# A two-layer graph network in float32 on one core: score products in another order, a second layer with 256 columns a graph, and a bias added by an accumulating transfer

## The chip, the cores and the metric

The kernel runs on one core of a Trainium2 chip. The time is that of the device for one execution, in microseconds (us). In the profile PE is TensorE, PEld its weight loads, DVE VectorE, ACT ScalarE, POOL GpSimd and SP the engine that issues most transfers.

## The reference

The input x has 64 graphs of 256 nodes with 512 features, adj a 256 x 256 weight matrix for each graph, all in float32. Two layers follow each other, each on a normed and rectified copy of x and added to x:

```python
h = maximum(layernorm(x), 0)
q, k, v = h @ Wq.T + bq, h @ Wk.T + bk, h @ Wv.T + bv
w = adj * exp(q @ k.T)
x = x + (w / w.sum(axis=2)) @ v

h = maximum(layernorm(x), 0)
A = adj + eye
d = A.sum(-1) ** -0.5
x = x + (A * d[:, None] * d[None, :]) @ (h @ W + b)
```

## The kernel before, in words

The kernel works on pairs of graphs (G = 2, NP = 32 pairs). A pair has four row blocks of 128 rows (TB = 4); block t = nb * G + g is row half nb of graph g. x of three pairs, and adj of two, are held in SBUF.

Every large product is done with seven products of half size instead of eight (a Winograd scheme): four quarters of each operand and sums of them go in, and sums of the products come out. `seven_products` (L342) does this for three stages, each with 28 matmuls of 128x128 by 256 columns: `key_side` (pm_g: h times the merged query and key weight), `values` (pm_v) and the second layer's weight product (pm_w). A product `product(bank, ...)` adds into one of three PSUM banks, 0, 1, 0, 1, 2, 1, 2 in this order, and between two uses of a bank a DVE or ACT operation reads it. The callbacks `then_first`, `then_u2`, `then_c11`, `then_u3` put other work on the engines behind the operation that reads the bank.

`attend` (L488) does the scores the same way, with products of 128 columns (pm_s, L500) in four banks. `first` (sA), `u2` and `u3` (sU) and `c22` (sC) are the sums on the way. `weights(kb, qb, scores)` then takes ACT's exponential (L519) for two graphs and multiplies on DVE by the transposed adjacency (L520, called the mask below); wT holds the result. The fourth part of `attend` multiplies wT by v (pm_o, L548), takes the reciprocal of the row sum (L556) and adds to x (L558). Because the row weights add up to one, the value bias can be added to x itself: `add_value_bias` (L738) does so before L558 with four additions on POOL (L741).

`transposed_adjacency` (L468) makes aT with DVE's 32x32 transposes from a copy of adj (aq) whose blocks a transfer has put in place; aT is laid out as (key half, query half, graph, query). After the first layer POOL adds the identity to aT's diagonal blocks (L801). `convolve` (L600 on) then forms pm_l (L611) with aT as the moving operand, 128 columns a matmul, two graphs side by side in a bank, and feeds the result as seven parts (yS) to pm_w. Its results are scaled by degree and added to x by DVE (L646) and POOL (L653).

Other names in the steps: `key_sums` (L329, gS) and `feature_sums` (L315, hS) make the operand sums, on POOL but for the first pair's hS; `weight_sums` (L155) makes those of a weight; `find_terms` calls `key_terms` (hc, L282), a row sum on DVE; `degrees` (L560) and `weighted_degrees` (ad, L579) give d; `scale_offset` (L245) measures mean and variance (L251) and ends in roots on POOL (L242); `normed` (L264) is ACT's normed copy h.

Each engine works through its own list in order. The order is that in which the program names the operations, except that `tc.issue_after(x)` puts what is named in it behind the instruction x, and that a planner (the tile framework) moves instructions of independent chains past each other when the program is built. In the middle of the program, for each pair p, the stages follow as attend(p), key side and values of p + 1, second layer of p; so pm_s, pm_o, pm_g, pm_v, pm_l, pm_w, and again. The start does key side and values of pair 0 with work of pair 1 among them (`project_first_pair`, L764), and the end has two second layers.

Of the kernel before, what the change touches and what calls it, by code (L numbers as in the profile page):

```python
# [9 lines left out]
F32 = mybir.dt.float32  # L10
# [6 lines left out]
def kernel(  # L17
# [93 lines left out]
    bkT = const.tile([P, DC], F32, tag="bkT", name="bkT")  # L111
    bv_all = const.tile([P, D], F32, tag="bv", name="bv_all")
    b1_all = const.tile([P, D], F32, tag="b1", name="b1_all")
# [14 lines left out]
    load_a(1)  # L128
    nc.sync.dma_start(bv_all, bv.partition_broadcast(P))
    w1_view = w1.rearrange("(j t p) (i f) -> i j p t f", p=P, t=2, f=HD)  # L130
# [198 lines left out]
    def key_sums(p, gT):  # L329

        a11, a21 = gT[:, 0:2, 0:N], gT[:, 0:2, N:NT]
        a12, a22 = gT[:, 2:4, 0:N], gT[:, 2:4, N:NT]
        gS = p1.tile([P, 3, 2, N], F32, tag="gS", name=f"gS_{p}")
        s1, s2, s4 = (gS[:, i] for i in range(3))
        nc.gpsimd.tensor_tensor(s1, a21, a22, add)
        nc.gpsimd.tensor_tensor(s2, s1, a11, sub)

        nc.gpsimd.tensor_tensor(a21, a11, a21, sub)
        nc.gpsimd.tensor_tensor(s4, a12, s2, sub)
        return (a11, a12, a22, s1, s2, a21, s4)  # L340
# [88 lines left out]

    def values(p, parts, then_first, then_u2, then_c11, then_u3):  # L430
        a1, s2, s3 = (temp(tag, f"v{p}") for tag in ("A1", "U2", "U3"))

        def block(i, g):
            return v[:, 2 * g : 2 * g + 2, i * (HD + 1) : i * (HD + 1) + HD]

        def first(pm):
            with tc.issue_after(nc.scalar.copy(a1, pm).ins):
                then_first()

        def u2(pm):  # L440
            with tc.issue_after(nc.vector.tensor_tensor(s2, pm, a1, add).ins):  # L441
                then_u2()

        def c11(pm):
            with tc.issue_after(nc.scalar.copy(block(0, 0), pm).ins):
                then_c11()

        def u3(pm):
            with tc.issue_after(nc.vector.tensor_tensor(s3, pm, a1, add).ins):  # L449
                then_u3()  # L450

        return seven_products(
            f"v_{p}",
            v_set,
            parts,
            True,
            first=first,
            u2=u2,
            c11=c11,
            u3=u3,  # L460
            c22=lambda pm: nc.vector.tensor_tensor(block(1, 1), pm, s3, add),
            c21=lambda pm: nc.vector.tensor_tensor(block(1, 0), pm, a1, add),
            c12=lambda pm: nc.vector.tensor_tensor(block(0, 1), pm, s2, add),
        )

    def transposed_adjacency(p):
        a = a_tiles[p]

        aT = p2.tile([P, NB, NB, G, P], F32, tag="aT", name=f"aT_{p}")
        if p > 0:  # L470
            in_view = q_tiles[p].rearrange("p kt (g j) r -> p kt g (j r)", g=G)
            for kt in range(NB):
                for g in range(G):
                    nc.vector.transpose(aT[:, kt, :, g, :], in_view[:, kt, g])
            return aT
        for g in range(G):
            pt = ps_m.tile([P, NB, NB, P], F32, tag="pm", name=f"pt_a_{p}_{g}")
            for kb in range(NB):
                for qb in range(NB):
                    nc.tensor.transpose(  # L480
                        pt[:, kb, qb, :], a[:, qb * G + g, ts(kb, P)], ident
                    )
            nc.scalar.copy(aT[:, :, :, g, :], pt)
        return aT

    def attend(p, h_parts, g_parts, ks, aT):
# [27 lines left out]

        def weights(kb, qb, scores):
            block = wT[:, kb, qb]
            for g in range(G):
                t = kb * G + g
                nc.scalar.activation(block[:, g], scores[:, g], AF.Exp, bias=ks[:, t : t + 1])  # L519
            nc.vector.tensor_tensor(block, block, aT[:, kb, qb], mult)  # L520

# [3 lines left out]
        nc.vector.tensor_tensor(u2, pm1, first, add)  # L525
        product(0, a12, b21, False)
        weights(0, 0, pm0)
        product(1, s3, t3, False)
        nc.vector.tensor_tensor(u3, pm1, first, add)
        pm2 = product(2, s1, t1)  # L530
        nc.vector.tensor_tensor(c22, pm2, u3, add)
        pm3 = product(3, a22, t4)
        nc.vector.tensor_tensor(u3, pm3, u3, add)
        weights(1, 0, u3)
        weights(1, 1, c22)
        product(2, s4, b22, False)
        nc.vector.tensor_tensor(u2, pm2, u2, add)
        weights(0, 1, u2)
        for qb in range(NB):
# [60 lines left out]
    def convolve(p, h, aT, d, moved, then_t4, then_first, then_u3):  # L600
# [4 lines left out]

        def aggregate(fh, qb):
            pm = ps_m.tile([P, 2, N], F32, tag="pm", name=f"pm_l_{p}_{qb}_{fh}")
            for fi in range(2):
                for g in range(G):
                    for jb in range(NB):  # L610
                        nc.tensor.matmul(  # L611
                            pm[:, fi, ts(g, P)],
                            h[:, jb * G + g, ts(2 * fh + fi, P)],
                            aT[:, jb, qb, g, :],
                            start=jb == 0,
                            stop=jb == NB - 1,
                        )
            return pm
# [17 lines left out]
        def block(i, g):  # L636
            return xt[:, 2 * g : 2 * g + 2, ts(i, HD)]

        def scaled(dst, pm, g, plus=None):

            for r in range(2):
                dr_ = d[:, 2 * g + r : 2 * g + r + 1]
# [50 lines left out]
        if p == NP - 1:  # L693
            for i, nb in ((0, 0), (1, 1), (1, 0), (0, 1)):
                rows = out[G * p : G * p + G, ts(nb, P), ts(i, HD)].rearrange("g p k -> p g k")
                nc.sync.dma_start(rows, block(i, nb))
        else:
# [40 lines left out]
    def add_value_bias(p):  # L738
        for t in range(TB):
            xh = x_tiles[p][:, t, :]  # L740
            nc.gpsimd.tensor_tensor(xh, xh, bv_all, add)  # L741

# [3 lines left out]
    def project(p, then_g):  # L746
        keys[p], last = key_side(p, parts[p], then_g, ahead(measure, p + 1), nothing)
        key_parts[p] = key_sums(p, keys[p])
        if p == 1:
            with tc.issue_after(last):  # L750
                weight_sums(w1_set, w1_21)
        last = values(
# [11 lines left out]
    def project_first_pair(v21):  # L764
# [6 lines left out]
        def during_g2():  # L771
            turn_blocks(1)
            deg[1] = degrees(1)
            with tc.issue_after(last_root[0]):
                add_value_bias(0)

        keys[0], _ = key_side(0, parts[0], lambda: norm_features(1), during_g, during_g2)
        key_parts[0] = key_sums(0, keys[0])
        last = values(
            0,  # L780
            parts[0],
            then_first=lambda: move_first_half(1),
            then_u2=lambda: find_terms(1),
            then_c11=lambda: move_second_half(1),
            then_u3=nothing,
        )
# [8 lines left out]
    def first_layer(p):  # L795
        attend(p, parts[p], key_parts[p], terms[p], aTs[p])


        for t in range(TB):
            diag = aTs[p][:, t // G, t // G, t % G]  # L800
            last = nc.gpsimd.tensor_tensor(diag, diag, ident, add)  # L801
# [107 lines left out]
```

## Time and profile before

| | us |
|---|---|
| median of 3 runs | 1868.14 |
| lowest and highest | 1866.42, 1868.26 |
| the profiled execution | 1865.99 |
| its span, first to last instruction | 1864.2 |
| PE busy, of the span | 1846.3 |
| DVE, POOL, ACT busy | 1346.6, 818.8, 802.2 |
| mean granted TensorE clock (1 is full) | 0.999 |

The page gives each engine's busy time and the costliest groups of instructions; the chain of waits follows the end of the program back to what released it; the timeline gives instructions in order of time. A float32 matmul of the program appears as two records. The ends of matmuls are modelled, so that their recorded length (379 ns for 256 columns) is longer than the distance of two of them; the distance is read from stretches of the chain. A wait is put down to the releaser that ended last in the records, which need not be the one that counted.

### The profile page before, as it was taken

The numbers are of one execution on the slowest core, as the hardware profiler recorded it, in microseconds if no ns is written. First come the engines' busy times: TensorE is split into PE (matmuls) and PEld (weight loads), VectorE is DVE, ScalarE is ACT, GpSimd is POOL, SyncE is SP. The second block draws the span as 40 slices with busy tenths as digits, with TensorE's granted clock in tenths as the row PEclk, the third lists the DMA queues.
The fourth block names the chain that finished last, engine by engine and source line by source line (L and its number), as shares of the span: only waits on it lengthen the run. The fifth ranks groups of instructions, "written<-read, shape, count | busy, mean of one in ns | idle before, by whom it ended". The sixth has DMA issues, their size and how long they took to land.

```text
span 1864.2 us, 28019 instructions
## 1 busy us (share of the span) xinstructions
PE 1846.3 (99%) x10370; PEld 1668.7 (90%) x10370; DVE 1346.6 (72%) x3160; ACT 802.2 (43%) x1476; POOL 818.8 (44%) x967
## 2 busy tenths in 40 slices
PE   9899999999999999999999999999999999999999
PEld 8799998999898999989998989999899989899988
DVE  6877777776776777777767767777777677677755
ACT  4344434344434444343444344444434443444422
POOL 3634345444345343454443453434544434534342
PEclk9999999999999999999999999999999999999999
DMA  8122022221122221222211222212222112222001
GB/s 209 29 74 74 23 57 73 70 74 49 43 63 68 74 74 23 57 74 69 74 49 43 63 69 74 74 23 57 74 69 74 49 44 63 68 74 74 7 23 46
DMA packets 207449, 115.14 MB, mean 62 GB/s; under 512 B 149712, under 2 KB 170192, under 8 KB 207312
## 3 DMA queue, kind: packets, MB, share of 16 engines
q1 hardware_dynamic: 206192, 112.29, 22.6%
q8 instruction: 82, 1.34, 0.3%
q14 instruction: 55, 0.45, 0.2%
q10 hardware_dynamic: 1056, 1.05, 0.2%
q0 software_dynamic: 64, 0.00, 0.1%
HBM read 79.70 MB, written 33.62 MB: 61 GB/s over the span
## 4 chain that ended last, share of the span: by engine, by line
PE 94%; DVE 3%; POOL 1%; ACT 1%; issue 1%; DVEq 0%; POOLq 0%
PE pm_g L359 21%; PE pm_w L359 21%; PE pm_v L359 20%; PE pm_l L611 12%; PE pm_o L548 12%; PE pm_s L500 7%; DVE wT L520 2%; POOL aT L801 1%; ACT wT L519 1%; PE pm_mT L177 1%; DVE hc L282 0%; PE pm_run_in L169 0%; DVE ad L579 0%; PE pt_h L302 0%; DVE w_set L157 0%
## 5 line engine op out<-in xcount | busy, mean ns | idle before, releaser
L359 PE MATMUL pm_w<-w_set,yS 128*128 128x256 f32 x1792 | 392.1, 379 | 0.0
L359 PEld LDWEIGHTS pm_w<-w_set,yS 128*128 128x128 f32 x1792 | 338.0, 190 | 44.6
L312 ACT COPY hT<-hq 32x512 f32<-32x512 f32 x496 | 305.5, 616 | 35.5 <-DVE hq L293 29.7
L653 POOL TENSOR_TENSOR x<-x,A_w 128x512 f32<-128x512 f32 x32 | 40.6, 1268 | 525.2 <-ACT A_w L644 525.2
L359 PE MATMUL pm_v<-v_set,hT 128*128 128x256 f32 x1024 | 242.0, 379 | 2.5 <-DVE U_v L441 2.5
L359 PE MATMUL pm_g<-hT,m_set 128*128 128x256 f32 x1024 | 236.7, 379 | 0.0
L611 PEld LDWEIGHTS pm_l<-aT,h_b 128*128 128x128 f32 x2048 | 233.7, 192 | 1.7
L611 PE MATMUL pm_l<-aT,h_b 128*128 128x128 f32 x2048 | 233.8, 275 | 0.0
L548 PE MATMUL pm_o<-v,wT 128*128 128x257 f32 (+1 forms) x1024 | 228.0, 379 | 0.4 <-DVE wT L520 0.4
L359 PEld LDWEIGHTS pm_v<-v_set,hT 128*128 128x128 f32 x1024 | 194.6, 190 | 29.4 <-DVE U_v L441 2.9
L359 PEld LDWEIGHTS pm_g<-hT,m_set 128*128 128x128 f32 x1024 | 194.5, 190 | 27.0 <-issue 0.5
L548 PEld LDWEIGHTS pm_o<-v,wT 128*128 128x128 f32 x1024 | 190.9, 189 | 27.5 <-DVE wT L520 1.4
L359 PE MATMUL pm_v<-v_set,hS 128*128 128x256 f32 x768 | 178.3, 382 | 3.4 <-DVE U_v L449 3.4
L359 PE MATMUL pm_g<-hS,m_set 128*128 128x256 f32 x768 | 181.3, 379 | 0.0
L359 PEld LDWEIGHTS pm_v<-v_set,hS 128*128 128x128 f32 x768 | 146.9, 191 | 23.8 <-DVE U_v L449 3.6
L741 POOL TENSOR_TENSOR x<-x,bv_all 128x512 f32<-128x512 f32 x128 | 164.5, 1313 | 0.0
L359 PEld LDWEIGHTS pm_g<-hS,m_set 128*128 128x128 f32 x768 | 145.4, 190 | 20.5 <-DVE U_g L399 0.3
L646 DVE SCALAR_TENSOR_TENSOR x<-pm_w,irr_d,x 128x256 f32<-128x256 f32 x256 | 110.9, 474 | 71.8 <-PE pm_w L359 71.8
L520 DVE TENSOR_TENSOR wT<-wT,aT 128x256 f32<-128x256 f32 x128 | 104.5, 816 | 52.8 <-ACT wT L519 52.8
L653 POOL TENSOR_TENSOR x<-x,U_w 128x512 f32<-128x512 f32 x64 | 81.3, 1270 | 105.6 <-DVE x L646 105.6
L268 ACT ACTIVATE h_b<-x,nb_b,rs_b 128x512 f32<-128x512 f32 x128 | 93.8, 803 | 62.6 <-POOL nb_b L261 62.6
L391 ACT COPY A_g<-pm_g 128x512 f32<-128x512 f32 x32 | 18.8, 586 | 232.9 <-PE pm_g L359 232.2
(137 smaller groups left out, 2688.5 us busy)
## 6 DMA issues: line engine op xcount, KB each, us to landing
x<-in_x_dram SPq DMA_DIRECT2D x64, 512.0 KB, 5.3
out_dram<-x SPq DMA_DIRECT2D x62, 512.0 KB, 3.5
a<-in_adj_dram SPq DMA_DIRECT2D x64, 256.0 KB, 2.9
aq<-in_adj_dram SPq DMA_DIRECT2D x124, 128.0 KB, 3.7
drow<-dflat SPq DMA_DIRECT2D x32, 256.0 KB, 4.8
wk_rows<-in_L_gnn_Wk_w_dram SPq DMA_DIRECT2D x2, 512.0 KB, 6.8
wq_rows<-in_L_gnn_Wq_w_dram ACTq DMA_DIRECT2D x2, 512.0 KB, 7.5
wv_rows<-in_L_gnn_Wv_w_dram SPq DMA_DIRECT2D x1, 1024.0 KB, 11.0
```

The source lines that it names most:

```text
L177: nc.tensor.matmul(pm, wk_rows[:, oc, ts(dc, P)], wq_rows[:, oc, ts(half, HD)], start=oc == 0, stop=oc == DC - 1,)
L268: nc.scalar.activation(h[:, t, :], x_tiles[p][:, t, :], AF.Relu, bias=nb[:, t : t + 1], scale=rd[:, t : t + 1],)
L312: last = nc.scalar.copy(dst[j * Q : (j + 1) * Q, i], src[i * Q : (i + 1) * Q, j])
L359: nc.tensor.matmul(banks[bank][:, r, :], left[:, ts(r, P)], right, start=start and r == 0 and dt == 0, stop=r == 1 and dt == 1, skip_group ...
L391: with tc.issue_after(nc.scalar.copy(a1, pm).ins):
L500: nc.tensor.matmul(banks[bank][:, g, :], left[:, dt, ts(g, P)], right[:, dt, ts(g, P)], start=start and g == 0 and dt == 0, stop=g == 1 an ...
L520: nc.vector.tensor_tensor(block, block, aT[:, kb, qb], mult)
L548: nc.tensor.matmul(pm[:, 0:width], wT[:, kb, qb, g, :], v[:, kb * G + g, lo : lo + width], start=kb == 0, stop=kb == NB - 1,)
L611: nc.tensor.matmul(pm[:, fi, ts(g, P)], h[:, jb * G + g, ts(2 * fh + fi, P)], aT[:, jb, qb, g, :], start=jb == 0, stop=jb == NB - 1,)
L646: last = nc.vector.scalar_tensor_tensor(dst[:, r, :], pm[:, r, :], dr_, plus[:, r, :], mult, add)
L653: last = nc.gpsimd.tensor_tensor(block(i, g), block(i, g), more, add).ins
L741: nc.gpsimd.tensor_tensor(xh, xh, bv_all, add)
```

## The change

The parts are these. `attend` takes the third bank's first product and the second bank's second one earlier, splits `weights` into exponentials and masks, and puts the masks behind the sums of later products. aT is laid out as (key half, graph, query), so that pm_l takes 256 queries of one graph in a matmul, with half as many matmuls, and a bank of pm_l holds one graph; the second layer's results belong to a graph instead of a row half. The value bias is added to x by one transfer from memory with an addition at its target, issued by POOL, instead of by four additions. In the start, the key sums of pair 0 go from POOL to DVE, those of the second layer's weight come from pair 1 forward into the values of pair 0, and find_terms(1) moves to the end of these.

```diff
-    bv_all = const.tile([P, D], F32, tag="bv", name="bv_all")
-    nc.sync.dma_start(bv_all, bv.partition_broadcast(P))
...
# key_sums
-        nc.gpsimd.tensor_tensor(s1, a21, a22, add)
+        eng = nc.vector if p == 0 else nc.gpsimd
+        eng.tensor_tensor(s1, a21, a22, add)
...
# values
+        def c22(pm):
+            with tc.issue_after(nc.vector.tensor_tensor(block(1, 1), pm, s3, add).ins):
+                then_c22()
...
# transposed_adjacency
-        aT = p2.tile([P, NB, NB, G, P], F32, tag="aT", name=f"aT_{p}")
+        aT = p2.tile([P, NB, G, N], F32, tag="aT", name=f"aT_{p}")
         if p > 0:
-            in_view = q_tiles[p].rearrange("p kt (g j) r -> p kt g (j r)", g=G)
             for kt in range(NB):
-                for g in range(G):
-                    nc.vector.transpose(aT[:, kt, :, g, :], in_view[:, kt, g])
+                nc.vector.transpose(
+                    aT[:, kt].rearrange("p g q -> p (g q)"),
+                    q_tiles[p][:, kt].rearrange("p j r -> p (j r)"),
+                )
...
# attend
-        def weights(kb, qb, scores):
-            block = wT[:, kb, qb]
+        def exponentials(kb, qb, scores):
             for g in range(G):
                 t = kb * G + g
-                nc.scalar.activation(block[:, g], scores[:, g], AF.Exp, bias=ks[:, t : t + 1])
-            nc.vector.tensor_tensor(block, block, aT[:, kb, qb], mult)
+                nc.scalar.activation(
+                    wT[:, kb, qb, g], scores[:, g], AF.Exp, bias=ks[:, t : t + 1]
+                )
+
+        def mask(kb, qb):
+            block = wT[:, kb, qb]
+            nc.vector.tensor_tensor(block, block, aT[:, kb, :, ts(qb, P)], mult)
 
         pm0 = product(0, a11, b11)
         nc.scalar.copy(first, pm0)
         pm1 = product(1, s2, t2)
         nc.vector.tensor_tensor(u2, pm1, first, add)
-        product(0, a12, b21, False)
-        weights(0, 0, pm0)
+        pm2 = product(2, s1, t1)
         product(1, s3, t3, False)
         nc.vector.tensor_tensor(u3, pm1, first, add)
-        pm2 = product(2, s1, t1)
-        nc.vector.tensor_tensor(c22, pm2, u3, add)
+        last = nc.vector.tensor_tensor(c22, pm2, u3, add)
+        product(0, a12, b21, False)
+        exponentials(0, 0, pm0)
+
+        with tc.issue_after(last.ins):
+            mask(0, 0)
         pm3 = product(3, a22, t4)
         nc.vector.tensor_tensor(u3, pm3, u3, add)
-        weights(1, 0, u3)
-        weights(1, 1, c22)
+        exponentials(1, 0, u3)
+        mask(1, 0)
+        exponentials(1, 1, c22)
         product(2, s4, b22, False)
-        nc.vector.tensor_tensor(u2, pm2, u2, add)
-        weights(0, 1, u2)
+        with tc.issue_after(nc.vector.tensor_tensor(u2, pm2, u2, add).ins):
+            mask(1, 1)
+        exponentials(0, 1, u2)
+        mask(0, 1)
...
# convolve
+        def aggregate(fh, g):
+            pm = ps_m.tile([P, 2, N], F32, tag="pm", name=f"pm_l_{p}_{g}_{fh}")
             for fi in range(2):
-                for g in range(G):
-                    for jb in range(NB):
-                        nc.tensor.matmul(
-                            pm[:, fi, ts(g, P)],
-                            h[:, jb * G + g, ts(2 * fh + fi, P)],
-                            aT[:, jb, qb, g, :],
+                for jb in range(NB):
+                    nc.tensor.matmul(
+                        pm[:, fi, :],
+                        h[:, jb * G + g, ts(2 * fh + fi, P)],
+                        aT[:, jb, g, :],
...
-            return xt[:, 2 * g : 2 * g + 2, ts(i, HD)]
+            return of_graph(xt, g)[:, :, ts(i, HD)]
...
# add_value_bias
-        for t in range(TB):
-            xh = x_tiles[p][:, t, :]
-            nc.gpsimd.tensor_tensor(xh, xh, bv_all, add)
+        nc.gpsimd.dma_start(
+            x_tiles[p],
+            bv.partition_broadcast(P).unsqueeze(1).broadcast_to([P, TB, D]),
+            accum_op=add,
+        )
...
# project
-        if p == 1:
-            with tc.issue_after(last):
-                weight_sums(w1_set, w1_21)
...
# project_first_pair
-            with tc.issue_after(last_root[0]):
-                add_value_bias(0)
+            add_value_bias(0)
+
+        def during_v():
+            key_parts[0] = key_sums(0, keys[0])
-        key_parts[0] = key_sums(0, keys[0])
             then_first=lambda: move_first_half(1),
-            then_u2=lambda: find_terms(1),
+            then_u2=during_v,
             then_c11=lambda: move_second_half(1),
-            then_u3=nothing,
+            then_u3=lambda: weight_sums(w1_set, w1_21),
+            then_c22=lambda: find_terms(1),
```

More of the change, by code (lines that the diff above doesn't have):

```diff
@@ L334, in key_sums @@
         s1, s2, s4 = (gS[:, i] for i in range(3))
-        nc.gpsimd.tensor_tensor(s1, a21, a22, add)
-        nc.gpsimd.tensor_tensor(s2, s1, a11, sub)
-        nc.gpsimd.tensor_tensor(a21, a11, a21, sub)
-        nc.gpsimd.tensor_tensor(s4, a12, s2, sub)
+        eng = nc.vector if p == 0 else nc.gpsimd
+        eng.tensor_tensor(s1, a21, a22, add)
+        eng.tensor_tensor(s2, s1, a11, sub)
+        eng.tensor_tensor(a21, a11, a21, sub)
+        eng.tensor_tensor(s4, a12, s2, sub)
         return (a11, a12, a22, s1, s2, a21, s4)
@@ L428, in key_side, with values @@
         return gT, last.ins
-    def values(p, parts, then_first, then_u2, then_c11, then_u3):
+    def values(p, parts, then_first, then_u2, then_c11, then_u3, then_c22=lambda: None):
         a1, s2, s3 = (temp(tag, f"v{p}") for tag in ("A1", "U2", "U3"))
@@ L460, in values @@
             u3=u3,
-            c22=lambda pm: nc.vector.tensor_tensor(block(1, 1), pm, s3, add),
+            c22=c22,
             c21=lambda pm: nc.vector.tensor_tensor(block(1, 0), pm, a1, add),
@@ L482, in transposed_adjacency @@
                     )
-            nc.scalar.copy(aT[:, :, :, g, :], pt)
+            nc.scalar.copy(aT[:, :, g, :], pt.rearrange("p kb qb q -> p kb (qb q)"))
         return aT
@@ L604, in convolve @@
         b11, b21, b22, t1, t2, t3, t4 = parts = [yS[:, i] for i in range(7)]
-        def aggregate(fh, qb):
-            pm = ps_m.tile([P, 2, N], F32, tag="pm", name=f"pm_l_{p}_{qb}_{fh}")
+        def aggregate(fh, g):
+            pm = ps_m.tile([P, 2, N], F32, tag="pm", name=f"pm_l_{p}_{g}_{fh}")
             for fi in range(2):
-                for g in range(G):
-                    for jb in range(NB):
-                        nc.tensor.matmul(
-                            pm[:, fi, ts(g, P)],
-                            h[:, jb * G + g, ts(2 * fh + fi, P)],
-                            aT[:, jb, qb, g, :],
-                            start=jb == 0,
-                            stop=jb == NB - 1,
-                        )
+                for jb in range(NB):
[3 more added lines that the diff above has]
+                        aT[:, jb, g, :],
+                        start=jb == 0,
+                        stop=jb == NB - 1,
+                    )
             return pm
@@ L636, in block @@
         def block(i, g):
-            return xt[:, 2 * g : 2 * g + 2, ts(i, HD)]
+            return of_graph(xt, g)[:, :, ts(i, HD)]
         def scaled(dst, pm, g, plus=None):
             for r in range(2):
-                dr_ = d[:, 2 * g + r : 2 * g + r + 1]
+                dr_ = d[:, r * G + g : r * G + g + 1]
                 if plus is None:
@@ L693, in convolve @@
         if p == NP - 1:
-            for i, nb in ((0, 0), (1, 1), (1, 0), (0, 1)):
-                rows = out[G * p : G * p + G, ts(nb, P), ts(i, HD)].rearrange("g p k -> p g k")
-                nc.sync.dma_start(rows, block(i, nb))
+            for i, g in ((0, 0), (1, 1), (1, 0), (0, 1)):
+                nc.sync.dma_start(in_dram(out, p, g)[:, :, ts(i, HD)], block(i, g))
         else:
@@ L738, in add_value_bias @@
     def add_value_bias(p):
-        for t in range(TB):
-            xh = x_tiles[p][:, t, :]
-            nc.gpsimd.tensor_tensor(xh, xh, bv_all, add)
+        nc.gpsimd.dma_start(
+            x_tiles[p],
+            bv.partition_broadcast(P).unsqueeze(1).broadcast_to([P, TB, D]),
+            accum_op=add,
+        )
     def nothing():
@@ L799, in first_layer @@
         for t in range(TB):
-            diag = aTs[p][:, t // G, t // G, t % G]
+            diag = aTs[p][:, t // G, t % G, ts(t // G, P)]
             last = nc.gpsimd.tensor_tensor(diag, diag, ident, add)
```

## The prediction

> **What bounds the kernel now.** I read the page's busy line first, then the chain of waits inside one middle pair, then the groups by shape, then the waits, and last the timeline of the places where the chain leaves TensorE.
>
> ```profile
> PE 1846.3 (99%) x10370; PEld 1668.7 (90%) x10370; DVE 1346.6 (72%) x3160; ACT 802.2 (43%) x1476; POOL 818.8 (44%) x967
> ```
>
> And the chain around one pair (start, length, what):
>
> ```profile
> 960.63 12.09 PE pm_w L359 x56
> 972.72 2.69 PE pm_s L500 x24
> ...
> 976.10 1.11 DVE wT L520
> ...
> 977.28 0.88 POOL aT L801 x2
> ...
> 978.21 1.13 PE pm_s L500 x8
> 979.34 6.93 PE pm_o L548 x32
> 986.27 8.63 PE pm_g L359 x40
> ...
> 1010.45 7.14 PE pm_l L611 x64
> ```
>
> TensorE is busy for 99% of the span, and the chain of one pair is one TensorE stage after another. One period, from pm_s at 915.76 to pm_s at 972.72, is 56.96 us. So time can come from two sources only: matmuls that get cheaper, and the few places where TensorE waits. The DVE and POOL steps in the chain (976.10 to 978.16) mostly run beside score matmuls. The chain passes through them only because the last score product was released late.
>
> The groups by shape (busy us, mean ns):
>
> ```profile
> L359 PE MATMUL pm_w<-w_set,yS 128*128 128x256 f32 x1792 | 392.1, 379 | 0.0
> L611 PE MATMUL pm_l<-aT,h_b 128*128 128x128 f32 x2048 | 233.8, 275 | 0.0
> L114 POOL DMA_DIRECT2D bqT<-in_L_gnn_Wq_b_dram x1 | 1.0, 987 | 0.8 <-POOLq L895 0.8
> ```
>
> The waits (total us, times, longest):
>
> ```profile
> PEld pm_s L500 <- POOL aT L801: 8.0, 29, 0.3
> PE pm_v L359 <- DVE U_v L449: 3.4, 1, 3.4
> PE pm_v L359 <- DVE U_v L441: 2.5, 1, 2.5
> ```
>
> The matmuls are recorded in two passes each. The pitch is read from the chain: pm_w 12.09 / 56 = 215.9 ns for 256 columns, pm_l 7.14 / 64 = 111.6 ns for 128, pm_s 2.69 / 24 = 112.1 ns. The waits say where TensorE stood: once a pair in the scores, and twice in the start, where a DVE addition came late.
>
> The timeline of the scores and masks (start, length):
>
> ```profile
> 977.64 0.42 DVE L531 TENSOR_TENSOR sC<-pm_s,sU 128x256 f32<-128x256 f32 x1
> 978.18 0.97 PEld L500 LDWEIGHTS pm_s<-hT,gS 128*128 128x128 f32 x8 [0.27 <-POOL aT L801]
> ...
> 980.41 5.14 POOL L741 TENSOR_TENSOR x<-x,bv_all 128x512 f32<-128x512 f32 x4
> 980.56 1.39 DVE L520 TENSOR_TENSOR wT<-wT,aT 128x256 f32<-128x256 f32 x1 [0.43 <-ACT wT L519]
> ```
>
> And one stretch of the start (busy, granted clock, DMA):
>
> ```profile
> 54.00:55.00 1.00, 1.00 (x4) 0.50 0.70 150
> ```
>
> The last score product adds into the bank that L531 reads. L531 ends at 978.06 and the product starts at 978.18, so L531 is the true releaser. The POOL step named has nothing that the product needs. The window row is the start: after TensorE stood until 52.58, its granted clock is 0.50 from 53 to 56.
>
> **The change, part by part.**
>
> *Second layer in 256 columns.* 64 passes of 128 columns become 32 of 256 in each pair, with the same operands. By the trace: 7.14 - 32 x 0.2159 = 0.23 us a pair. A rule of the Trainium skill ("TensorE: Matmul & The Clock Gate", Back-to-back issue gap) gives a matmul its array cycles at 2.4 GHz plus about 2.5 ns; with two cycles a column, which fits 215.9, 128 columns should take 109.2 ns and the gain would be 64 x 0.1092 - 6.91 = 0.08 us. The trace has 111.6, so I take 0.23: x 32 = 7.4 us (by the rule 2.6). The weight load (190 ns) stays hidden under 215.9. What follows pm_l (sums for L359 pm_w) has about 2 us to spare. The adjacency transposes become two of 128x512 (678 ns by L293) instead of four of 411 ns: 0.29 us less DVE, off the path.
>
> *Scores in another order.* The stage pm_s takes 6.62 us in the chain and 56 x 0.112 = 6.27 without waiting: 0.35 us a pair. In the new order (products 0, 1, 2, 1', 0', 3, 2') with e = 0.90 us a product from 972.56: product 1' ends at 976.16, the two sums u3 and c22 end at about 977.35 (0.25 us to start, as L525 shows, then 2 x 0.42 and a gap), and 2' needs them at 977.96. So that wait goes. What is late next is the masks. exp(0,0) runs 977.24 to 977.87 (product 0' ends 977.06), mask(0,0) at 0.42 us ends 978.32; the first pm_o wants it at about 978.65. The build's order puts mask(1,0) on DVE behind u2, which waits for 2' (978.86): u2 979.11 to 979.53, mask(1,0) to 979.97. The fourth pm_o matmul needs it at 978.86 + 3 x 0.433 = 980.16, its weights 0.2 earlier. That is a wait of 0 to 0.15 us. Both figures hold if the masks take 0.42; they take 1.1 to 1.4 when POOL holds them up (L520 at 976.10 and 980.56). POOL's hS sums end at 976.92 and its diagonal additions (0.88 us) fall between the two masks, so I take 0.42. Net gain 0.30 us (0.2 to 0.35) x 30 pairs = 9.0 us.
>
> *Value bias by an accumulating transfer.* Four POOL additions (5.14 us a pair) become one transfer of 1 MB, issued by POOL in the same place, behind the diagonal additions. No row shows such a transfer. Issue: the nearest row is L114, 512 pieces like this one, 0.99 us. A rule speaks against the move: the skill ("SBUF — State Buffer", SBUF: two separate sides) says that descriptors made by GpSimd wait while DVE holds the shared port, and a 620 ns transfer then takes about 3100. By the row the issue costs 1 us on POOL, by the rule some 3.5. Behind it in POOL's queue stand the L240 roots of the second norm; they wait for DVE until 988.49 in any case, and the additions that go covered until 985.55. So both prices are zero on the path, and I use the row. It would have to take over 6 us to delay L240, and about 6 us more before A_v (L437, behind h_b on ScalarE) held up TensorE. No DVE operation beside it reads two SBUF tensors. Landing: the x loads take 5.3 us for half the bytes; even 30 us lies well inside the 57 us until the next pair's L558 wants x. It starts near 982 when the x load is nearly in (977.84 + 6); that x is first read at 990.44. Nothing is queued behind it on SP. Bounds: gain 0 (POOL was not on the path), loss 0 unless the issue passes 12 us.
>
> *The start.* Pair 0's key sums go to DVE (4 x 0.69, pitch 0.62), the w1 sums come forward from pair 1, find_terms(1) moves behind c22, and bv_all's load goes. In pair 1 the w1 sums cost 1.77 us each against POOL and made TensorE wait 2.5 us: pair 1 takes 59.67 (72.22 to 131.89) instead of 56.96, so 2.7 us go. In pair 0, from 47.73 to 72.05, the work is 17.5 us and 6.8 are lost: 3.4 of waiting, 1.8 at half clock, 0.65 before L500 at 62.5 and 0.9 among pm_o. Set out anew on DVE: key sums until 48.2, U3 until 48.9 (TensorE needs it at 48.8), three w1 sums, c22 until 51.4 (needed at 51.35): 0.25 lost. Then w1, four hc, c21, c12, two transposes and one ad stand before the first score sum. Uncontended it ends at 58.1, with POOL's hS sums beside it (hc took 1.64 beside POOL) at 60.1; TensorE wants it at 56.85. So 1.4 to 3.3 us come back there, and 1.2 more where u3 and c22 follow at once. I take 4.5 lost instead of 6.8. Gain of the start 2.7 + 2.3 = 5.0 (2.7 if the late wait halves the clock again, 6.5 at best). The first accumulating transfer stands ahead of pair 1's roots on POOL (free 23.4 to 24.67 before); at the rule's price these come some 2 us late, and h_a's first reader is at 36.84.
>
> *The end.* The four last stores keep size and order: nothing.
>
> **Sum.** 7.4 + 9.0 + 5.0 = 21.4 us. The profiled execution took 1865.99 (span 1864.2), so it should take 1844.6; the median of the runs is 1868.14, 2.1 above it, and by that 1846.7.
>
> **Rivals.** (1) The wait in the scores moves to the masks: pm_o waits about as long for mask(1,0) as 2' did for c22. For it: 0.1 us of margin in my own working. Against it: POOL is idle at that moment. Gain 7.4 + 5.0 = 12.4, time 1855.7. (2) Wide matmuls pay by the rule, and nothing else changes: 2.6 + 9.0 + 5.0, time 1851.5. Against it: three groups with one pitch. (3) Slower: both masks meet POOL. If the diagonal addition overlaps mask(1,0) and the hS sums overlap mask(0,0), at 1.39 and 1.10 us, pm_o starts 0.35 late and its fourth matmul another 1.0: 1.35 lost a pair in place of 0.35. 30 x 1.0 - 7.4 - 5.0 = +17.6, time 1885.7. It decides against the change from about 0.75 us of waiting a pair. Against it: POOL's sums end 1 us before mask(0,0), by the same TensorE clock in both kernels. (4) The transfer does not do what it says off the path: its 1 MB delays x loads by over 6 us, bn_stats (L251) at 990.44 waits, and L399, behind it on DVE, holds pm_g. The engines are idle from 984 to 997, which speaks against. At 1 us a pair late: 30 - 21.4 = +8.6, time 1876.7.
>
> **How the numbers follow.** Forecast 0.68, of which the own range is 1843 to 1850 (terms 10.5 and 6.5 at best; 6 and 2.7 at worst). Rival 1: 0.15. Rival 2: 0.08. Rival 3: 0.05. Rival 4: 0.04. The range reaches over rivals 1 and 2 to 1857 and, for starts and issues that go better than worked out, down to 1840. About 0.2% (3.7 us) is what a measurement of this kernel can tell from no change. Forecast and rivals 1 and 2 are all faster by more than that, 0.91; rivals 3 and 4 are slower, mostly by more, 0.06 after some of both falls near zero, 0.03.
>
> **What would show it.** Right: pm_l as 1024 records in about 221 us; the chain's pair at 56.4 us; no wait of pm_s on L531's successor; masks all near 0.42 us; POOL 160 us less busy, with issues near 1 us; no long wait of pm_v at 49 and at 90, a new one of 1 to 3 us at the second score product of pair 0. Wrong: pm_o waiting for a mask in every pair; issues over 6 us on POOL, or POOL's L240 starting after 990 in the pair's clock; bn_stats waiting for x; a half clock near 60.

## The result, and the profile after

| us | before | after |
|---|---|---|
| median of 5 runs, on one chip | 1866.59 | 1846.23 |
| lowest and highest | 1866.27, 1868.26 | 1845.12, 1846.69 |
| the profiled execution | 1865.99 | 1845.12 |
| its span | 1864.2 | 1843.3 |

The ratio of the mean times is 0.9887, 95% interval 0.9873 to 0.9902; the medians lie 20.4 us apart. Between the two profiled executions it is 20.9 us, against 21.4 in the forecast's sum.

The busy line of the changed kernel's page:

```profile
PE 1831.0 (99%) x9346; PEld 1632.8 (89%) x9346; DVE 1297.7 (70%) x3102; ACT 801.7 (43%) x1476; POOL 690.0 (37%) x867
```

There are 1024 matmul records fewer (16 matmuls of the program less in each pair, two records each), and POOL is 129 us less busy: 164 us of additions went and 43 us of issues came, and pair 0's key sums are DVE's now. TensorE is still busy for 99% of the span, so POOL's and DVE's savings did not pay as such. The chain of waits around one pair (start, length, what) shows where the time went:

```profile
997.85 6.91 PE pm_l L625 x32
...
1016.85 6.27 PE pm_s L504 x56
```

pm_l takes 6.91 us instead of 7.14, and the scores are one unbroken piece of 6.27 where they took 6.62 with a detour over ACT, DVE and POOL. The other stages have their old lengths. The period of a pair falls from 56.96 to 56.38 us, and the whole middle of the program consists of it. The waits of TensorE (total us, times, longest):

```profile
PE pm_s L504 <- DVE sU L533: 2.5, 1, 2.5
PE pm_s L504 <- DVE sC L537: 2.3, 2, 1.6
```

The two long waits of pm_v are gone. What is left, the run-in aside, is two waits of pm_s, both in the start, with a small third (0.62 us) in the last pair. How far the start has come shows in the chain where pm_g of pair 1 starts, and then that of pair 2; before, and then after:

```profile
72.22 8.63 PE pm_g L359 x40
...
131.89 8.63 PE pm_g L359 x40
```

```profile
71.74 8.63 PE pm_g L358 x40
...
128.12 8.63 PE pm_g L358 x40
```

Pair 0 gained 0.5 us, pair 1 3.3, of which 2.7 are the wait that went and 0.6 are what every pair gains.

In the timeline of one pair, the sum that released the last score product late before, that product's weights, and the masks:

```profile
1020.93 0.42 DVE L537 TENSOR_TENSOR sC<-pm_s,sU 128x256 f32<-128x256 f32 x1
...
1021.95 0.97 PEld L504 LDWEIGHTS pm_s<-hT,gS 128*128 128x128 f32 x8
...
1023.55 1.22 DVE L528 TENSOR_TENSOR wT<-wT,aT 128x256 f32<-128x256 f32 x3
```

sC ends at 1021.35, 0.6 us before the weights of the last product are loaded: that load has no wait any more. The masks behind it take 1.22 us for three. The issues of the transfers of all pairs, as one group (nanoseconds: least, median, most); POOL does one in the place of the four additions, and it lands after 9.8 us (median):

```profile
L752 POOL DMA_DIRECT2D x<-in_L_gnn_Wv_b_dram x32: 1329/1338/1392, 23.5 to 1758.3; - x32
```

### The profile page after: what moved, and what is told of

The parts are those of the page before. It is cut to its first block, busy times and chain, and to the rows that moved or that the text cites. A ratio compares the mean times of both kernels' runs of the same rounds, so it can differ in the third digit from the quotient of the medians.

```text
span 1843.3 us, 25928 instructions
## 1 busy us (share of the span) xinstructions
PE 1831.0 (99%) x9346; PEld 1632.8 (89%) x9346; DVE 1297.7 (70%) x3102; ACT 801.7 (43%) x1476; POOL 690.0 (37%) x867
## 3 DMA queue, kind: packets, MB, share of 16 engines
q10 hardware_dynamic: 1056, 1.05, 0.2%
## 4 chain that ended last, share of the span: by engine, by line
PE 97%; DVE 1%; DMA 1%; issue 0%; POOL 0%; ACTq 0%; DVEq 0%
PE pm_w L358 21%; PE pm_g L358 21%; PE pm_v L358 20%; PE pm_o L562 12%; PE pm_l L625 12%; PE pm_s L504 11%; PE pm_mT L175 1%; DMA wq_rows<-in_L_gnn_Wq_w_dram 1%; DMA dflat<-irr_d 0%; DVE hc L280 0%; DVE ad L593 0%; DVE hq L291 0%; PE pt_h L300 0%; PE pt_wv L225 0%; DVE deg L578 0%
## 5 line engine op out<-in xcount | busy, mean ns | idle before, releaser
L625 PE MATMUL pm_l<-aT,h_b 128*128 128x256 f32 x1024 | 226.2, 379 | 0.0
L625 PEld LDWEIGHTS pm_l<-aT,h_b 128*128 128x128 f32 x1024 | 194.6, 190 | 26.5
L572 DVE SCALAR_TENSOR_TENSOR x<-pm_o,rsum,x 128x256 f32<-128x256 f32 x256 | 110.5, 473 | 2.0 <-DVE rsum L570 1.1
L436 ACT COPY A_v<-pm_v 128x512 f32<-128x512 f32 x32 | 18.7, 585 | 206.1 <-PE pm_v L358 197.1
```

The costliest lines, as they stand in the source:

```text
L572: nc.vector.scalar_tensor_tensor(xh, pm[:, 0:HD], rsum, xh, mult, add)
L625: nc.tensor.matmul(pm[:, fi, :], h[:, jb * G + g, ts(2 * fh + fi, P)], aT[:, jb, g, :], start=jb == 0, stop=jb == NB - 1,)
```

## Experiments

Every ratio below is against runs of the kernel before that were timed beside it. The changed kernel was not timed beside them. The intervals of most of its variants overlap with its own, so a difference from it of up to about 3 us rests on the stage times of the profiles and not on the medians.

### Each part alone

Four kernels, each the kernel before with one part of the change. First the matmuls of 256 columns (the aT layout, `aggregate` by graph, the second layer's results by graph), nothing else:

```diff
-                for g in range(G):
-                    for jb in range(NB):
-                        nc.tensor.matmul(pm[:, fi, ts(g, P)], ..., aT[:, jb, qb, g, :])
+                for jb in range(NB):
+                    nc.tensor.matmul(pm[:, fi, :], ..., aT[:, jb, g, :])
```

> The kernel before with the second layer by graph alone (aT laid out by graph, 256 columns a matmul, results by graph). Theory (the parts add, each worth what its own stage shows): pm_l 6.91 us a pair instead of 7.14, 32 x 0.235 = 7.5 us off, about 1859.1. Rival by the rule of columns / 2.4 GHz + 2.5 ns: 2.6 us off, about 1864. Rival that the parts need each other: no clear gain, since the score stage waits as before.

Measured: 1854.33 us, ratio 0.9934 (0.9921 to 0.9946), 12.9 below the median of before: more than forecast. Its chain gives the reason: besides pm_l at 6.91, the score stage takes 6.49 us, though the score code is the old one.

```profile
968.80 6.49 PE pm_s L501 x56
```

By the timelines the 0.13 us come from the transposes (no kernel was run with these alone changed). In the old order mask(0,0) stands on DVE ahead of the sums that release the last product, and it is slow while POOL makes the hS sums. These stand on POOL behind an addition to x (L653), which waits for a DVE operation (L646), which stands behind the adjacency transposes. The timeline of before, and then that of this kernel:

```profile
968.37 1.41 DVE L474 STREAM_TRANSPOSE aT<-aq 128x256 f32<-128x256 f32 x4
...
970.62 1.27 POOL L653 TENSOR_TENSOR x<-x,U_w 128x512 f32<-128x512 f32 x1 [3.32 <-DVE x L646]
```

```profile
964.45 1.29 DVE L472 STREAM_TRANSPOSE aT<-aq 128x512 f32<-128x512 f32 x2
...
966.58 1.27 POOL L653 TENSOR_TENSOR x<-x,U_w 128x512 f32<-128x512 f32 x1 [3.20 <-DVE x L646]
```

Two transposes take 0.12 us less than four, POOL's row starts 1.94 us before pm_s (972.56) in the one and 2.06 (968.64) in the other, and the mask, which began at the same distance from pm_s, takes 0.98 us (972.17 on) instead of 1.10 (976.10 on). So 7.4 + 30 x 0.13 = 11.3 us. The two profiled executions are 9.7 us apart (spans 1864.2 and 1854.5), because TensorE lost 1.7 us in pair 1 to a half clock that the profile of before does not have there (last section); what the medians have over 11.3 lies within the scatter of before's runs on this chip (1866.0 to 1868.6). In the whole change this is no gain of its own: there mask(0,0) is behind the sums, and the wait is gone with or without it.

Second, the score order with the masks behind sums alone (`attend` as in the diff):

> The kernel before with the new order of score products, sums and masks alone; POOL still adds the value bias. Theory: the wait for c22 goes in 30 pairs, 30 x 0.35 = 10.5 us off, and the last pair gives about 0.8 back: about 1856.9; all masks near 0.42 us, because POOL's additions start behind the last diagonal addition and the last mask has then begun. Rival (entangled parts): the masks meet POOL's additions, mask mean stays above 0.7 us and pm_o waits: gain under 4 us.

Measured: 1858.61, ratio 0.9952 (0.9938 to 0.9965), 8.6 less than before. In the middle pairs all 0.35 us of the stage come (6.27 us in one piece), and no mask takes over 0.50. All masks as one group (ns):

```profile
L524 DVE TENSOR_TENSOR wT<-wT,aT x128: 412/425/501, 65.1 to 1807.1; 128x256 f32<-128x256 f32 x128
```

30 x 0.35 is 10.5. Two pairs take some of it back: pair 0 loses 1.34 us (pm_g of pair 1 at 73.56 instead of 72.22), and the last pair 0.76 (14.26 us from pm_s to pm_l instead of 13.50). In both DVE comes late to the first score sum, and the sums u3 and c22 then follow too close on product 1'.

Third, the transfer alone:

> The kernel before with the accumulating transfer alone in place of POOL's four additions. Theory: POOL is about 120 us less busy and the last mask of a pair falls from 1.39 to 0.42 us, but neither is on the path: within 1.5 us of before, 1865 to 1867, what there is coming from the start. Rival (POOL's additions slowed the masks that pm_o waits for): 30 x 0.3 = 9 us off.

Measured: 1866.38, ratio 0.9998 (0.999 to 1.0006). Nothing, as forecast: POOL's additions were not on the path.

Fourth, the changes of the start alone:

> The kernel before with the changed start alone (key sums of pair 0 on DVE, sums of the second weight in the values of pair 0, find_terms(1) last). Theory: pair 1 loses its 2.5 us wait (2.7 off); pair 0 gains nothing, since POOL's additions to pair 0 (until 48 us) now slow the key sums on DVE to about 1.6 us each in place of hc: 1863 to 1865. Rival (the start is worth by itself what the sum gave it): 5 us off, 1861.6.

Measured: 1866.27, ratio 0.9996 (0.9988 to 1.0004). Pair 1 gains all of its 2.7 us: pm_g to pm_g takes 56.96 us (74.56 to 131.52) instead of 59.67. But 74.56 is 2.34 us later than before: pair 0 gives it back. The key sums are on DVE now, and POOL's four bias additions run beside them (timeline):

```profile
42.75 5.42 POOL L746 TENSOR_TENSOR x<-x,bv_all 128x512 f32<-128x512 f32 x4
...
47.07 1.64 DVE L337 TENSOR_TENSOR gS<-gS,gT 128x512 f32<-128x512 f32 x1
48.64 0.68 DVE L339 TENSOR_TENSOR gT<-gT 128x512 f32<-128x512 f32 x1
```

The first two sums take 1.23 and 1.64 us beside POOL, the third 0.68 alone.

### All but the transfer

If that is so, the transfer is worth something in the start after all. In the changed kernel the four additions take its place again:

```diff
...
-        nc.gpsimd.dma_start(x_tiles[p], bv....broadcast_to([P, TB, D]), accum_op=add)
+        for t in range(TB):
+            xh = x_tiles[p][:, t, :]
+            nc.gpsimd.tensor_tensor(xh, xh, bv_all, add)
```

> The changed kernel with the four POOL additions of the value bias back in place of the accumulating transfer. Theory: in the middle pairs the transfer is worth nothing (alone it gave 0.9998), but in the start POOL's additions stand beside the key sums that the change puts on DVE, which cost start_only 2.34 us in pair 0; so pair 0 loses about 2.5 us again against the changed kernel (pm_g of pair 1 near 74.3 instead of 71.74), and the time is about 1848.8 (1847.5 to 1850). Rival: the transfer is worth nothing here either, 1846.2. Second rival: the additions also meet the masks, which now come later, in every pair: over 1 us a pair is not excluded by the page alone, 1855 or more.

Measured: 1848.14, ratio 0.9897 (0.988 to 0.9913), 1.9 more than the changed kernel. pm_g of pair 1 starts at 74.53 instead of 71.74, and the next period is 56.37. Part of these 2.8 us is the clock: it is at half for 6.8 us from 62.4 on instead of 3.4. So the transfer pays in pair 0 and nowhere else. The masks do not meet the additions.

### The start and the end, mended

In the start the changed kernel's profile shows what is left of the lost time (timeline of pair 0; then stretches of 1 us with length, PE busy and its records, granted clock, DMA share and GB/s):

```profile
59.21 1.16 PE L504 MATMUL pm_s<-hT,gT 128*128 128x128 f32 x8 [2.54 <-DVE sU L533]
...
60.73 0.42 DVE L593 SCALAR_TENSOR_TENSOR ad<-a,drow 128x256 f32<-128x256 f32 x1
...
61.08 0.42 DVE L536 TENSOR_TENSOR sU<-pm_s,sA 128x256 f32<-128x256 f32 x1
...
62.01 2.07 PE L504 MATMUL pm_s<-hT,gS 128*128 128x128 f32 x8 [1.64 <-DVE sC L537]
```

```profile
63.00:64.00 1.00, 1.00 (x7) 0.50 0.91 298
...
65.00:66.00 1.00, 1.00 (x5) 0.78 1.13 178
```

TensorE stands for 2.54 us and, after one product, for another 1.64; then it runs at half clock from 62.0 until about 65.4 (0.78 is the mean of the last stretch). About 1.7 us more go there: 3.4 us at half speed. Two pieces of DVE work stand ahead of the late sums that nobody needs yet: the transposes of pair 1 and the degree weights (ad, L593) of pair 0. The next kernel is the changed one with both later:

```diff
+        if p == 1:
+            with tc.issue_after(last):      # the key side of pair 1
+                weigh_degrees(0)
...
-        with tc.issue_after(last.ins):      # the values of pair 0
-            weigh_degrees(0)
...
-        aTs[1] = transposed_adjacency(1)
         first_layer(0)
+        aTs[1] = transposed_adjacency(1)
```

> The changed kernel with two pieces of pair 0's DVE work moved behind what TensorE waits for: the transposes of pair 1's adjacency behind pair 0's attention, and the degree weights of pair 0 behind the key side of pair 1. Theory: of the start's 2.3 us that I forecast for pair 0 only 0.5 came, because DVE reaches the first score sum of pair 0 2.5 us late and the c22 sum 1.6 us late, and TensorE then runs at half clock for about 3 us (1.6 us lost). About 3.4 us of DVE work leaves the queue ahead of that sum, so both waits and the half clock should go: 4 us less than the changed kernel (3 to 5.7), about 1842.2, and pair 1's pm_g starts near 68 instead of 71.74. Rival: what delays the sum is the contention with POOL's hS sums and not the queue; then less than 1.5 us come back, 1845 or more.

Measured: 1844.63, ratio 0.9881 (0.9866 to 0.9896), 1.6 less than the changed kernel, not 4. Pair 0 gains 3.6 us (pm_g of pair 1 at 68.13), the half clock at 62 is gone, and pair 1 loses 3.2. The degree weights now stand ahead of U_v beside POOL's gS sums:

```profile
81.50 1.36 DVE L593 SCALAR_TENSOR_TENSOR ad<-a,drow 128x256 f32<-128x256 f32 x1
...
82.66 1.34 POOL L335 TENSOR_TENSOR gS<-gS,gT 128x512 f32<-128x512 f32 x1
...
87.70 1.99 PE L358 MATMUL pm_v<-v_set,hT 128*128 128x256 f32 x8 [2.31 <-DVE U_v L440]
```

Three of the four take 1.36 to 1.38 us there, and 0.42 where POOL is idle. The wait was moved and the work made dearer. So the degree weights went to an earlier place, between the key side's sums of pair 1 and ahead of POOL's gS sums:

```diff
+        then_u3 = (lambda: weigh_degrees(0)) if p == 1 else nothing
-        keys[p], last = key_side(p, parts[p], then_g, ahead(measure, p + 1), nothing)
+        keys[p], last = key_side(p, parts[p], then_g, ahead(measure, p + 1), then_u3)
```

> As late_start, but the degree weights of pair 0 stand in the key side of pair 1 between its sums, ahead of POOL's gS sums, and not behind them. Theory: late_start gained 3.6 us in pair 0 and lost 3.2 of it in pair 1, where the four products took 1.38 us each beside POOL's gS sums (0.42 alone) and held up U_v, so that TensorE waited 2.3 and 0.4 us; between 75.8 and 80.3 us DVE stands for 2.7 us and POOL does nothing, and there they take 2.2. Expected 3 us less than late_start's 1844.6: 1841.5 (1840.8 to 1843), pair 1 from pm_g to pm_g 56.4 and no wait of pm_v. Rival: pm_g's last blocks come late instead, and pm_g or pm_s waits about 1 us or more: 1843 to 1845.

Measured: 1841.17 (1841.15 to 1841.31), ratio 0.9861 (0.9844 to 0.9877), 5.1 us less than the changed kernel. In its chain:

```profile
67.79 12.10 PE pm_g L358 x56
...
124.17 8.63 PE pm_g L358 x40
```

The degree products take 0.41 to 0.43 us, pm_g runs through, and pair 1 takes 124.17 - 67.79 = 56.38 us like all others. Pair 0 alone is 3.95 us shorter than in the changed kernel, and the spans differ by 3.9 (1839.4 against 1843.3); the medians differ by more because the profiled execution is the shortest of the changed kernel's five. This is the fastest kernel of the study.

For the end, late_start with the graph bias of the pair before moved behind the last attention:

```diff
-        with tc.issue_after(last.ins):
-            add_graph_bias(p - 1)
+        if p < NP - 1:
+            with tc.issue_after(last.ins):
+                add_graph_bias(p - 1)
...
+            add_graph_bias(p - 1)           # after first_layer of the last pair
```

> As late_start, and in the last pair the graph bias of the pair before moves behind the last attention. Theory: the last pair's score stage took 14.27 us from pm_s to pm_l in the changed kernel and 13.50 before, because the 2.73 us of graph bias on DVE stand ahead of the first score sum and u3 and c22 then follow at once. Expected 0.8 us less than late_start: about 1841.4, last stage 13.5 or less. Rival: the graph bias only shows up again at the end, in front of the last outputs: 0 less than late_start, or up to 2 us more.

Measured: 1845.03, ratio 0.9882 (0.9868 to 0.9897): nothing over late_start. The last score stage is whole again (13.20 us from pm_s to pm_l), but the planner moved the first bias addition ahead of a sum of the key side, and TensorE waits there for 1.05 us:

```profile
1767.69 0.75 DVE L610 SCALAR_TENSOR_TENSOR x<-b_all,ds,x 128x512 f32<-128x512 f32 x1 [3.08 <-ACT h_b L266]
...
1769.19 1.97 PE L358 MATMUL pm_g<-hT,m_set 128*128 128x256 f32 x8 [1.05 <-DVE U_g L394]
```

### How much room the masks have

The first rival moved the wait to the masks. Useless DVE additions were put between the last score sum and mask(1,0) of the changed kernel, one in mask_late and two in mask_late2:

```diff
-        mask(1, 0)
...
+            extra = nc.vector.tensor_tensor(small("sJ"), u2, first, add)
+        with tc.issue_after(extra.ins):
+            mask(1, 0)
             mask(1, 1)
```

> The changed kernel with one added DVE addition of 128x256 (about 0.42 us with its gap 0.46) between the last score sum and mask(1,0); its result is used by nothing. It measures how much room is left before rival 1 of the prediction (the wait moves to the masks) comes true. In the changed kernel mask(1,0) ends about 0.85 us after the first pm_o matmul starts and the fourth wants it at 1.1, so 0.25 us are free, and the addition makes pm_o wait about 0.2 us a pair: 6 us more, about 1852 (1848 to 1856). If the room were only the 0.1 us of the prediction: 0.35 a pair, 1857. Rival: no pm_o matmul is near to waiting for a mask, 1846.2.

Measured: 1846.14, ratio 0.9888 (0.9874 to 0.9903): nothing. But the planner had put a fourth pm_o matmul ahead of those that read mask(1,0), where the changed kernel has three. With that the mask is wanted 0.43 us later, as much as the addition takes, so this run does not measure the room in the old order. The trace of the changed kernel does. mask(1,0) is the first of the three masks shown above and ends at 1023.97. The first weight load that needs it:

```profile
1024.05 0.19 PEld L562 LDWEIGHTS pm_o<-v,wT 128*128 128x128 f32 x1
```

The room is 0.08 us, not the 0.25 that was expected, and it is 0.07 to 0.08 in every middle pair.

> As mask_late, with two added DVE additions (0.85 us together) ahead of mask(1,0). With one, nothing was lost: the planner put a fourth pm_o matmul of the first half ahead of those that read mask(1,0), so that they want it 0.43 us later. With two, the order stays that, mask(1,0) ends about 1.65 us after the first pm_o matmul starts, and the fifth wants it at 1.73, its weights about 0.2 earlier. Theory: pm_o waits 0.1 to 0.2 us in each pair, 3 to 6 us more than the changed kernel's 1846.2: about 1850.5 (1849 to 1853). Rival: the weights may be loaded as late as the matmul itself starts and there is room still, 1846.2.

Measured: 1851.91, ratio 0.9915 (0.9899 to 0.9932), 5.7 more than the changed kernel, in the middle of what was expected. pm_o is 7.11 us long in the chain instead of 6.93, and its weight loads wait for the mask in nearly every pair (total us, times, longest):

```profile
PEld pm_o L566 <- DVE wT L528: 9.6, 31, 0.3
```

So the price of the first rival is real: the second addition, 0.42 us against a room of 0.1, costs 0.18 a pair. In the changed kernel mask(1,0) comes in time, but only just.

### How much room the issue has

The transfer of a pair was cut into 8 and into 16, to lengthen POOL's issue:

```diff
+        for t in range(TB):
+            for c in range(2):              # 4 in the other
+                nc.gpsimd.dma_start(x_tiles[p][:, t, ts(c, 256)],
+                                    bv[ts(c, 256)].partition_broadcast(P), accum_op=add)
```

> The changed kernel with the transfer of each pair cut into 8 accumulating transfers of 128 KB (the same bytes into the same x). It makes POOL's issue longer, to see how much room there is behind it: the roots of the second norm (L238, L240) stand next in POOL's queue, 5.03 us after the issue ends in the changed kernel. Theory: 8 issues of 1.0 to 1.34 us end 8 to 11 us after the start, the roots come 1.6 to 4.4 us late, and since ScalarE is free between h_b and A_v TensorE does not wait: 1846.2, no change (within 2 us). Rival (the skill's rule that descriptor writing by GpSimd starves): more than 1.5 us an issue, the roots over 6 us late and some us more in every pair, over 1870.

Measured: 1847.21, ratio 0.9892 (0.9878 to 0.9907), no wait of TensorE in the middle pairs and the period 56.37; 0.8 of the 1.0 us over the changed kernel lie in pair 0 (pm_g of pair 1 at 72.56). The eight issues take 7.20 us, and the roots start 0.9 us late against pm_s (15.86 us after it instead of 14.96). That is less than expected, since an issue takes 0.9 us and not 1.0 to 1.34.

> As split_8, with 16 transfers of 64 KB: POOL issues for 16 to 21 us. Theory: the roots come 9.6 to 15 us late, h_b ends 2 to 8 us after A_v (behind it on ScalarE) should start, and TensorE waits 2 to 8 us in each of 31 pairs: 1910 to 2090. This is the price of the cover that the prediction named (12 us from the start of the issue). Rival: the delay is taken up elsewhere, less than 1 us a pair, below 1877.

Measured: 1876.04, ratio 1.0045 (1.0029 to 1.0061): slower than before. The period is 57.25 us in the mean (57.18 in the pair below), 0.87 more, and pair 0 loses 3.6 us. By its size this is the rival's case, by its mechanism the theory's with a shorter issue: 14.31 us a pair instead of 16 to 21. The timeline of one pair, and then the chain there:

```profile
985.75 14.31 POOL L754 DMA_DIRECT2D x<-in_L_gnn_Wv_b_dram  x16
...
1000.13 0.23 POOL L238 TENSOR_SCALAR irs_b<-mv_b 128x4 f32<-128x4 f32 x1
```

```profile
1003.80 0.50 ACT h_b L266
...
1005.92 0.48 ACT A_v L436
...
1006.45 8.90 PE pm_v L358 x40
```

The roots wait for POOL's queue, h_b for the roots, A_v for h_b on ScalarE, and TensorE for A_v. With 0.87 us lost at 14.3, the room ends at about 13.4 us, an estimate from this one point; the prediction had put it at 12.

## Why the prediction was right, point by point

| step | forecast, us | in the profiles, us |
|---|---|---|
| pm_l in 256 columns | 7.4 | 32 x (7.14 - 6.91) = 7.4 |
| scores, middle pairs | 9.0 | 30 x (6.62 - 6.27) = 10.5 |
| start, pair 1 | 2.7 | 59.67 - 56.96 = 2.7 |
| start, pair 0 | 2.3 | 72.22 - 71.74 = 0.5 |
| scores in the last pair | in "the end: nothing" | 13.50 - 14.27 = -0.8 |
| transfer | 0 | 0 in the middle; see below |
| sum | 21.4 | 20.3, of 20.9 between the spans |

What is missing in the last line is 0.3 us after the last matmul and roundings of the stage lengths, which count thirty times. The mechanisms were right but for the terms below; that the sum lies within 0.5 us of the forecast is in part luck, since the scores gave 1.5 us more than was taken and pair 0 and the last pair 2.6 less.

*The matmuls* came as worked out from the chain's own pitch. The rule of the Trainium skill ("TensorE: Matmul & The Clock Gate", Back-to-back issue gap), with two cycles a column, would have made it 2.6 us and the second rival true. pm_l of 256 columns keeps the rule's pitch (6.91 / 32 = 0.2159), but 128 columns took 111.6 ns and not 109.2; the measurement decides, and the page itself gives its formula for an isolated matmul and says that it counts too little for small ones in a stream. The step called the transposes "off the path". In the old score order they are not, as wide_only shows; it cost the forecast nothing, because the new order takes that path away.

*The scores* were better than the value taken, because the 0 to 0.15 us of mask wait did not come. mask(1,0) was forecast to end 7.41 us after the first score product, from three masks of 0.42. It ended at about 7.3 (1023.97 less 1016.68), and pm_o did not wait. The first rival missed by little: with 0.08 us of room, as narrow as the 0.1 of the prediction's working, one addition beyond what a changed order of pm_o took up brought it about (mask_late2, 0.18 us a pair).

*The transfer* had its issue at 1.34 us, between the row (0.99) and the rule's 3.5 and much nearer to the row: in the records of all 32 it is never over 1.39. The Trainium skill ("SBUF — State Buffer", SBUF: two separate sides) tells of a DVE that holds the shared port; at this place of the kernel DVE has no operation that reads two SBUF tensors, so these runs do not speak against the rule, they only lie outside it. It landed in 9.8 us, x loads took 4.9 instead of 5.3, and no bn_stats waited: the fourth rival has no trace. What the prediction did not see is that the transfer is needed in the start: it takes POOL's additions from beside the key sums that the same change puts on DVE. Its sum for pair 0 had these sums uncontended without saying to which part that is due; alone, the transfer gives nothing and the start gives nothing.

*The start of pair 0* is the term that was mis-sized: 0.5 us came of 2.3. The forecast let 4.5 us stay lost in pair 0 (its terms add up to 2.9 to 4.8), and 6.3 did. The first score sum was forecast between 58.1 and 60.1 and ended at 59.15, so that wait, 2.54 us, was within the bounds. The second wait, "1.2 more where u3 and c22 follow at once", was 1.64: they do not follow at once, since three more degree products (L593) stand between sU and them on DVE, and u3 starts at 61.08. The larger part is the half clock, which the sum of 4.5 put at nothing and the prediction named only beside it ("2.7 if the late wait halves the clock again": start 3.2 measured). It came at 62.0 for 3.4 us and cost 1.7; "a half clock near 60" was one of the prediction's own signs of being wrong, and in this term it was. late_mid shows what this DVE work was worth: with it out of the way the waits are 0.5 and 1.0 us, the clock stays full, and pair 0 is 3.95 us shorter.

*The end*: stores cost nothing, but the last pair's scores were not looked at. There is no second layer ahead of them, the graph bias (2.73 us on DVE) stands before the first score sum, and the new order, which brings 1' close behind it, is 0.77 us worse than the old. scores_only shows the same 0.76 with none of the other parts.

*The third rival* (masks meet POOL) fell as argued: POOL's hS sums end 1.1 us before mask(0,0), and the slowest mask of all 128 groups takes 0.50 us, where before it was 1.40.

## What to carry to other kernels

A wait that a chain puts on one engine may be set three engines back: by the timelines 0.12 us less of transposes shortened a score stage by 0.13, over POOL's queue and a contended mask. Work that nobody needs yet belongs where the engine that slows it is idle, not merely later: the same degree products cost 0.42 us in one place and 1.38 in another, and moving them cost pair 1 what pair 0 had gained. Parts of a change can be worth nothing alone and something together, so each part's sum should say which other part it leans on. A wait of TensorE has a second price, the clock after it, and a forecast that names this price should also say why it does or does not charge it.

## What the runs showed of the hardware

TensorE's clock after a wait was not a matter of the wait's length alone. In before and in wide_only, TensorE stands in pair 1 for the same wait of U_v (2.46 and 2.45 us) and starts again at about 92. The one kept the full clock; the other ran at 0.50 for 3.4 us, and its pm_v took 8.86 us for 32 matmuls instead of 7.17: 1.7 us.

The traces show what made the difference. In all fourteen (before, after and the twelve kernels above), the granted clock changes only on a grid of 3.41 us: a stretch at half clock is 3.41 or 6.83 us long, and those at full clock before one are whole multiples of 3.41. Cut along that grid (stretch, length, PE busy and its records, granted clock, DMA share and GB/s), the place reads in before, and then in wide_only:

```profile
86.78:90.19 3.41, 2.70 (x13) 1.00 0.06 2
90.19:93.61 3.42, 1.67 (x8) 1.00 0.00 0
93.61:97.02 3.41, 3.41 (x18) 1.00 0.22 77
```

```profile
85.58:88.99 3.41, 3.41 (x17) 1.00 0.05 2
88.99:92.40 3.41, 0.96 (x5) 1.00 0.00 0
92.40:95.81 3.41, 3.41 (x10) 0.50 0.36 76
```

In before the wait falls on a border of the grid and is shared by two steps, in which TensorE is busy for 0.79 and 0.49 of the time. In wide_only it falls into one step and leaves 0.28. Over the fourteen traces this divides without an exception: after each of the 13 steps at full clock in which TensorE was busy for 0.42 or less, the next ran at half clock; after a step of 0.43 or more, none did. The nearest pair is late_both and late_start, with the same wait of 2.31 us in pair 1 and steps of 0.42 and 0.44: the first lost the clock, the second kept it. Once at half clock, a step busy for 0.58 to 0.73 kept it there, and a step busy throughout ended it. The Trainium skill ("TensorE: Matmul & The Clock Gate", Part 1: The HAM clock gate) says that the gate watches a free-running window of about 3.4 us, and these steps agree with it; a step without any work was not needed here. Where the grid lies against the program differed from trace to trace, so a wait of 2 to 3 us cost 1.7 us more in one and nothing in another.

In the start of the changed kernel the same reading gives:

```profile
58.61:62.03 3.42, 1.18 (x9) 1.00 0.24 38
62.03:65.44 3.41, 3.41 (x12) 0.50 0.94 221
```

TensorE was busy for 0.34 of the first of these steps. Had the second wait been the 1.2 us of the prediction, it would have been 0.47, and by the division above the clock would have stayed full: an estimate from these figures, not a run. late_mid, whose waits there are 0.5 and 1.0 us, has no step under 0.71 around them. Its four runs lie within 0.16 us of each other, the 25 of before on one chip within 2.6.

Elementwise work of DVE on SBUF tensors is slower beside POOL's: a 128x512 sum took 1.23 to 1.64 us beside POOL's additions and 0.68 alone, a 128x256 degree product 1.38 and 0.42. An accumulating transfer costs POOL 0.9 us to issue for 64 KB or 128 KB and 1.34 for 1 MB, so its price is mostly by transfer and little by byte.
